# Four layers of a graph transformer on one core: the last target products of a GATv2 layer moved into the next, edge fields fetched a group sooner, and weight loads placed behind gathers

## The chip, the cores and the metric

The kernel runs on one core of one Trainium2 chip. The metric is device time in microseconds (us), the median of three runs. Everything is computed in 32-bit floating point; a matmul of such numbers is made of two passes of TensorE.

The engines are named as in the profile: PE is TensorE (PEld its weight loads), DVE is VectorE, ACT is ScalarE, POOL is GpSimd and SP is SyncE, which here only issues transfers. SP, ACT and POOL each issue DMAs, and each works through its instructions in order.

## The reference

A graph of 1,250 nodes with 512 features each and 21,250 edges goes through four layers. Each layer adds a graph part (gnn) and an attention part (mix) to x, and then a mixture of experts (ffn). The four layers differ in kind. This is the end of the reference, with arguments left out:

```python
xn = layernorm(x)
x = x + L0_gnn(xn, ...) + L0_mix(xn, ...)
x = x + L0_ffn(layernorm(x), ...)
xn = layernorm(x)
x = x + L1_gnn(xn, ...) + L1_mix(xn, ...)
x = x + L1_ffn(layernorm(x), ...)
...
xn = layernorm(x)
x = x + L3_gnn(xn, ...) + L3_mix(xn, ...)
x = x + L3_ffn(layernorm(x), ...)
```

Three of its pieces are touched by the change. `L0_gnn` is itself a stack of three GATv2 layers (k = 0, 1, 2), which the text calls GAT layers 0, 1 and 2:

```python
for k in range(Wl.shape[0]):
    xl = x @ Wl[k] + bl[k]
    xr = x @ Wr[k] + br[k]
    ef = ea2 @ We[k]
    m = jax.nn.leaky_relu(xl[src2] + xr[dst2] + ef, SLOPE)
    logit = m @ att[k]
    alpha = _segment_softmax(logit, dst2, n)
    out = jax.ops.segment_sum(xl[src2] * alpha[:, None], dst2, num_segments=n) + b_out[k]
    h = out + x
    ...                                   # layernorm of h, scaled by gamma, shifted by beta
    x = jax.nn.relu(h)
```

`L1_mix` is a global attention with the weights Wq, Wk, Wv, W1 and W2. `L3_gnn` is a graph convolution (`h = x @ W`, gathered by edge, weighted and summed by target), and `L3_mix` a linear attention whose projection `w_qkv` is three matrices of 512 x 512:

```python
q = softmax(x @ Wq.T) * dim ** -0.5       # L1_mix
k = softmax(x @ Wk.T, axis=-2)
x = einsum(q, einsum(k, x @ Wv.T)) + x
return x @ W1.T @ W2.T + x
...
q, k, v = split(x @ w_qkv.T, 3)           # L3_mix, per head
q = elu(q * SCALE) + 1; k = elu(k) + 1
out = einsum(q, einsum(k, v)) / (einsum(q, k.sum(axis=2)) + 1e-08)
return out @ w_out.T + b_out
```

The mixture of experts at the end of layer 0 writes its experts' outputs to a table in memory, from which every node gathers two rows; that of layer 2 does so too.

## The kernel before

**Nodes and edges.** The nodes are ten tiles of 128 rows (NT = 10). For the GAT layers they are also cut into twelve blocks of 107 (BN, NB). The edges (with a second self loop for each node) are sorted by target into 188 edge tiles of 128 (FT). Four tiles make a group (GE), so there are 47 groups (FG), about four to a block.

**A GAT layer** (`gat_layer`, L1209). Two tables in memory hold the products of the nodes with Wl (by source, `tl`, shown as xl) and Wr (by target, `tr`, shown as xr, stored as two halves of reduced precision). For an edge tile i, step i of the loop does the following.

- `load` gathers the source rows of a whole group by indirect DMA on POOL (L231), three groups ahead. At the start of a block it also loads the block's target rows, on SP.
- `fields` loads for a group a compressed table of targets, nb, and the edge attributes into the lower rows of the tile oh, both on SP, two groups ahead. There are four buffers of nb and three of oh.
- `onehot` (L1273, ACT) makes from nb the matrix that picks the target of each edge, one group ahead.
- `right` (L1286, L1287, PE) multiplies that matrix with the target rows into a PSUM bank. `logits` adds the source rows (L1299, DVE, the tile s) and reduces with the attention vector (L1302). For part of the tiles PE adds the source rows instead.
- `spread` makes one row of logits per group (z). When a block is full, `turn` (L1340, L1343) and `mix` (L1353, PE, bank `more`) sum the weighted source rows of the block.

A finished block is normed (L1371 to L1403, DVE and ACT), stored (L1096), transposed by `across` (L1409, L1415), and for every node tile that is then complete the two products of the *next* layer are queued in `late`: `gat_tables` has four matmuls with Wl (L1166), the copy on ACT (L1171), a reduction on DVE (L1182, `left`) and the store to tl (L1184); then four with Wr, a copy (L1174), a subtraction (L1188, `right`) and the store to tr (L1189). They use the PSUM bank called `tab`; `right` uses three banks called `mm`. The queues `todo`, `edge` and `late` give one piece of work to each step of the loop; after the last edge tile a loop empties them.

`prepare` loads the vectors of the layer and the weights of the next layer. It is moved on by one piece every third step, from step 6.

**The frame.** The order of instructions on an engine is not that of the source: a scheduler orders each engine's instructions by its own simulated times, transfers included, unless a part is marked to keep its written order. Buffers come from pools, and an instruction that reuses a buffer waits for its last reader.

```python
    def weight(self, src, k, n):
        w = self.wp.tile([128, k, n], F32, tag="w", name="w")
        self.nc.sync.dma_start(w, src.rearrange("(k p) n -> p k n", p=128))
        return w
```

This helper (L138) loads a weight of 512 x 512, 1 MB, on SP (L141).

**The end of layer 0's ffn** (`layer0_ffn`). Each expert's output tile is stored on ACT's queue (L1781, 256 KB, l0moe_out); then 20 gathers (L231, tile g) fetch two rows per node, `add_scaled` adds them to x (L1811), and `norm_tile` and `transpose_tile` prepare the input of layer 1. The next function, `global_attention` (L1814), begins with the loads of WkT, WvT, WqT and W1.

**The start of layer 3** (`layer3_attn`, L2929). `tail_steps` (L2377) gathers the two expert rows per node of layer 2 (routed_out, tile g, added to z at L2887), norms, scales (L2896 on ACT, L2897 on POOL), adds to x, norms again and transposes (L2386, L2388), tile by tile. Beside it run the products with gnn_W (L171), whose results are scaled (L2945) and stored as gcn_h (L2946) for the gathers of the graph convolution. `linear_attention_steps` (L734) loads the three parts of w_qkv and scales wq on ACT (L762).

Of the kernel before, what the change touches and what calls it, by code (L numbers as in the profile page):

```python
# [24 lines left out]
D = 512  # L25
NT = 10
# [31 lines left out]
class Net:  # L58
# [76 lines left out]
        else:  # L135
            self.nc.vector.tensor_copy(out, psum)

    def weight(self, src, k, n):  # L138

        w = self.wp.tile([128, k, n], F32, tag="w", name="w")  # L140
        self.nc.sync.dma_start(w, src.rearrange("(k p) n -> p k n", p=128))  # L141
        return w

# [588 lines left out]


    def linear_attention_steps(self, xn, xT, w_qkv, w_out, b_out, qscale, finish, added=None,  # L734
                               need=None):

# [10 lines left out]

        with self.tc.tile_pool(name="la", bufs=1) as p, \  # L750
                self.tc.tile_pool(name="latmp", bufs=2) as tmp:
            wk = self.weight(w_qkv[:, D:2 * D], 4, D)
            wv = self.weight(w_qkv[:, 2 * D:3 * D], 4, D)
            bo = self.rowvec(b_out)

            P = p.tile([128, 4, D], F32, name="P")
            ks = p.tile([128, D], F32, name="ks")
            for half in range(2):
                if half:
                    wq = self.weight(w_qkv[:, 0:D], 4, D)  # L760
                    if qscale != 1.0:
                        nc.scalar.mul(wq, wq, qscale)  # L762
# [24 lines left out]
            kv = tmp.tile([128, D], F32, tag="r", name="kv")  # L787
            for f in range(4):
                fs = slice(f * 128, (f + 1) * 128)
                m = self.mm([128, 128])  # L790
                for c in range(4):
                    nc.tensor.matmul(m, lhsT=wv[:, c, fs], rhs=P[:, c, fs], start=c == 0,
                                     stop=c == 3)
                nc.vector.tensor_tensor(kv[:, fs], m, self.pair, op=ALU.mult)
            for f in range(4):
                m = self.mm()
                nc.tensor.matmul(m, lhsT=kv[:, f * 128:(f + 1) * 128], rhs=wo[:, f, :],
                                 start=True, stop=True)
                self.evac(kvo[:, f, :], m)
            yield  # L800
            Q, QT = {}, {}
            for i in range(NT + 2):
                if i < NT:
                    r = rows(i)
                    nc.gpsimd.tensor_tensor(self.x[:r, i, :], self.x[:r, i, :], bo[:r],
                                            op=ALU.add)
                    q = tmp.tile([128, D], F32, tag="q", name="q")
                    phi(q, self.nat(xT, wq, i))
                    prod = tmp.tile([128, D], F32, tag="r", name="prod")
                    nc.vector.tensor_tensor(prod, q, ks, op=ALU.mult)  # L810
                    den = tmp.tile([128, 8], F32, tag="den", name="den")
                    nc.vector.tensor_reduce(den, prod.rearrange("p (h d) -> p h d", h=8), AX.X,
                                            ALU.add)
                    finish(den, den)
                    nc.vector.reciprocal(den, den)
                    q8 = q.rearrange("p (h d) -> p h d", h=8)
                    nc.vector.tensor_tensor(q8, q8, den.unsqueeze(2).to_broadcast([128, 8, 64]),
                                            op=ALU.mult)
                    Q[i] = q
                if 1 <= i <= NT:  # L820
                    qT = tmp.tile([128, 4, 128], F32, tag="qT", name="qT")
                    self.transpose_tile(qT, Q.pop(i - 1))
# [386 lines left out]
    def gat_layer(self, L, p, xtab, otab, big):  # L1209
# [25 lines left out]
        edge = deque()  # L1235
        late = deque()
        step = [0]

        def block(g):
            return g // 4, g % 4, g % 4 == 3 or g == FG - 1  # L1240
# [12 lines left out]
            G.setdefault(g, {})["xl"] = xl  # L1253

        def fields(g):
            nb = p.tile([128, GE * 128], BF16, tag="nb", name="nb", bufs=4)
            nc.sync.dma_start(nb, self.nbt[g])
            s = p.tile([128, GE * 128], F32R, tag="oh", name="oh", bufs=3)
            nc.sync.dma_start(s[BW:K].bitcast(F32),
                              self.eat[:, g * GE * 128:(g + 1) * GE * 128])  # L1260
            G.setdefault(g, {}).update(nb=nb, s=s)
# [99 lines left out]
        def finish(b):  # L1361
# [44 lines left out]
            def across():  # L1406
# [8 lines left out]
                    nc.scalar.copy(X[t][:, :, lo - t * 128:hi - t * 128],  # L1415
                                   q[:, :, lo - r0:hi - r0])
                for t in whole:
                    for f in self.gat_tables(nxt, p, t, lambda c, t=t: X[t][:, c, :],
                                             lambda: self.bank("tab", [128, D])):
                        late.append((step[0] + 1, f))  # L1420

            def add(t):
# [33 lines left out]
        for g in range(3):  # L1456
            load(g)
        fields(1)
        onehot(0)
        prepared = prepare()  # L1460
        for i in range(FT + 3):
            g, j = divmod(i, GE)
            step[0] = i
            if j == 1:
# [3 lines left out]
                    load(g + 3)  # L1468
                if g + 1 < FG:
                    onehot(g + 1)  # L1470
            if j == 2 and g + 2 < FG:
                fields(g + 2)
            if i >= 6 and i % 3 == 0:
                next(prepared, None)
            if i % 16 == 8 and i < FT:
                load_cur(i // 16)
# [15 lines left out]
            if late and late[0][0] <= i and (i % 2 == 0 or len(late) > 8):  # L1492
                late.popleft()[1]()
        bias_cur(NB - 1)
        while edge or todo or late:
            for _ in range(2):
                if edge:
# [32 lines left out]
    def layer0_ffn_to_layer1_attn(self):  # L1530
# [11 lines left out]
        with self.tc.tile_pool(name="l1a", bufs=1) as p:  # L1542
            xnT = p.tile([128, 4, NP], F32, name="xnT")
            with self.tc.tile_pool(name="l1b", bufs=1) as pb:
                xn = pb.tile([128, NT, D], F32, name="xn")
                with self.weights(), self.psum(3, 2, 3) if fast else self.psum():
                    count_pool()
                    self.counting = self.count_blocks(range(CB), True) if fast else iter(())
                    self.layer0_ffn(xn, xnT)
# [7 lines left out]
                    self.global_attention(xn, xnT, steps)  # L1557
                    for _ in steps:
                        pass
            count_ctx.close()  # L1560
# [88 lines left out]
    def layer0_ffn(self, xn, xnT):  # L1649
# [6 lines left out]
        with self.tc.tile_pool(name="l0f", bufs=1) as p, \  # L1656
# [113 lines left out]
            for e in range(8):  # L1770
# [3 lines left out]
                while (done + 1) * 128 <= (e + 1) * RM:  # L1774
# [5 lines left out]
                    self.evac(o.rearrange("p (f d) -> p f d", f=4), q)  # L1780
                    nc.scalar.dma_start(obuf[done * 128:(done + 1) * 128, :], o)  # L1781
                    done += 1
            for t in range(NT):
                for j in range(2):
                    g = tmp.tile([128, D], F32, tag="g", name="g", bufs=6)
                    self.gather(g, obuf[:, :], getI[:, t, j:j + 1])
                    self.add_scaled(t, g, G[:, t, j:j + 1])
                self.ready(t)
                self.norm_tile(t, xn[:, t, :])
                self.transpose_tile(xnT[:, :, t * 128:(t + 1) * 128], xn[:, t, :])  # L1790
                self.count(1)
            g1.close()

    def clear(self, p):

# [15 lines left out]
        self.nc.vector.scalar_tensor_tensor(x, psum[:r], gate[:r], x, op0=ALU.mult, op1=ALU.add)  # L1811


    def global_attention(self, xn, xnT, steps):  # L1814


        nc, I = self.nc, self.I
        with self.tc.tile_pool(name="ga", bufs=3) as big, \
# [26 lines left out]
            wv = self.weight(I["L1_mix_WvT"], 4, D)  # L1845
            P = large([128, NT, D])
            for f in range(4):
                c = self.mm()
# [1080 lines left out]
    def layer3_attn(self):  # L2929
        nc, I = self.nc, self.I  # L2930
        added = self.both_added()
        with self.tc.tile_pool(name="l3", bufs=1) as p:
            xnT = p.tile([128, 4, NP], F32, name="xnT")
            xn = p.tile([128, NT, D], F32, name="xn")
            need = self.tail_steps(xn, xnT)
            th = self.dram.tile([NP, D], F32, name="gcn_h")
            H = self.dram.tile([NP, D], F32, name="gcn_sum")
            dinv = self.dinv
# [9 lines left out]
            with self.tc.tile_pool(name="gcn", bufs=2) as tmp:  # L2948
# [3 lines left out]
                else:  # L2952
# [2 lines left out]
                steps = self.linear_attention_steps(  # L2955
                    xn, xnT, I["L3_mix_w_qkvT"], I["L3_mix_w_outT"], I["L3_mix_b_out"], 0.125,
                    lambda o, d: nc.vector.tensor_scalar(o, d, 1e-8, None, op0=ALU.add),
                    added)

                W, HL = {}, {}  # L2960

# [296 lines left out]
```

## Time and profile before

| | us |
|---|---|
| median of 3 runs | 4464.39 (4461.85 to 4471.24) |
| profiled execution, own time | 4489.82 |
| profiled execution, span | 4487.9 |
| PE busy | 3922.2 (87%) |
| DVE busy | 2689.5 (60%) |
| ACT busy | 1622.8 (36%) |
| POOL busy | 1351.0 (30%) |
| first gather of GAT layers 0, 1, 2 | 319.7, 758.6, 1184.8 |

The profile is one execution, and it was slower than the median of the runs. Busy shares are means over stages that are very different: the GAT layers keep PE busy nearly throughout, while PE stands still where one layer's gathers wait for the stores of the layer before. A row of the timeline gives the start, the busy time of the instruction or of a run of like ones, engine, line, operation, the tile written and the tiles read, the count, and in brackets how long the engine had been idle and what ended that. The granted clock is the share of full speed that TensorE was allowed; at 0.50 a pass takes twice as long.

### The profile page before, as it was taken

To read this page: it belongs to the slowest core of one execution; us is meant where nothing else is said; L and a number is where in the kernel's file an instruction comes from. 1 tells how busy PE (TensorE), PEld (TensorE's weight loads), DVE (VectorE), ACT (ScalarE), POOL (GpSimd) and SP (SyncE) were. 2 spreads that over 40 slices of the span, in tenths; PEclk is the share of its full clock that TensorE was granted. 3 is DMA by queue.
4 is the path that set the end of the run, shared out by engine and by line. 5 is a ranking of instruction groups with operands and counts; after the bars stand their busy time and mean duration, and the time that the engine had idled before them with its cause. 6 is when DMAs were issued, how large, how long until landed. Compare 5 with 4: busy or idle time off the path is not lost. (4 is left out here: it accounts for less than half of the span.)

```text
span 4487.9 us, 49486 instructions
## 1 busy us (share of the span) xinstructions
PE 3922.2 (87%) x15466; PEld 2415.7 (54%) x15466; DVE 2689.5 (60%) x6338; ACT 1622.8 (36%) x2976; POOL 1351.0 (30%) x1308
## 2 busy tenths in 40 slices
PE   5987998899788867799999999997979896898796
PEld 3434554455354434444788877563546562455474
DVE  5357895888398865523896767314584225687301
ACT  2222442344133375110464446223451232554121
POOL 2017773776466501102000000103131013675102
PEclk9988999999899988899999999999989998997798
DMA  6437664666466423402421110383002653666695
GB/s 220 159 84 211 198 199 150 198 197 193 141 179 189 145 74 108 119 17 64 146 70 42 46 35 29 143 298 128 12 27 83 233 189 119 182 200 199 225 339 181
DMA packets 283001, 647.58 MB, mean 144 GB/s; under 512 B 61673, under 2 KB 108905, under 8 KB 267322
## 3 DMA queue, kind: packets, MB, share of 16 engines
q1 hardware_dynamic: 169290, 357.13, 24.1%
q0 software_dynamic: 73088, 234.75, 18.3%
q10 hardware_dynamic: 40352, 52.44, 3.4%
q8 instruction: 127, 2.08, 0.2%
q14 instruction: 144, 1.18, 0.1%
HBM read 528.87 MB, written 120.65 MB: 145 GB/s over the span
## 5 line engine op out<-in xcount | busy, mean ns | idle before, releaser
L231 POOL DMA_INDIRECT xl<-xl,srcI x564 | 616.8, 1094 | 290.2 <-issue 137.8
L1353 PE MATMUL more<-xl,wT 128*128 128x512 f32 x1128 | 579.7, 601 | 14.5 <-ACT wT L1343 14.0
L1286 PE MATMUL mm<-hl,oh 121*128 121x512 f32 x564 | 419.1, 743 | 73.8 <-DVE s L1299 37.8
L1302 DVE SCALAR_TENSOR_TENSOR junk<-s,att 128x512 f32<-128x512 f32 x534 | 417.9, 783 | 6.8
L1299 DVE TENSOR_TENSOR s<-xl,mm 128x512 f32<-128x512 f32 x534 | 357.8, 679 | 104.0 <-PE mm L1287 48.4
L2129 PE MATMUL more<-hh,e 128*128 128x259 f32 x1600 | 383.7, 385 | 11.7 <-ACT o L2072 8.6
L2129 PEld LDWEIGHTS more<-hh,e 128*128 128x128 f32 x1600 | 295.1, 191 | 75.8 <-issue 17.8
L171 PE MATMUL mm<-w,xnT 128*128 128x512 f32 x640 | 307.8, 620 | 16.6 <-ACT xnT L2388 12.1
L231 POOL DMA_INDIRECT hs<-gcn_h,srcI x188 | 214.6, 1142 | 93.6 <-issue 30.8
L1353 PEld LDWEIGHTS more<-xl,wT 128*128 128x128 f32 x1128 | 196.1, 192 | 74.8 <-issue 27.9
L1287 PE MATMUL mm<-hl,oh 121*128 121x512 f32 x564 | 236.4, 419 | 0.0
L1286 PEld LDWEIGHTS mm<-hl,oh 121*128 121x128 f32 x564 | 111.0, 197 | 215.5 <-issue 117.1
L231 POOL DMA_INDIRECT g<-routed_out,getI x60 | 67.6, 1126 | 488.5 <-DMA routed_out<-o 416.4
L2049 ACT ACTIVATE e<-r,hh 128x512 f32<-128x512 f32 (+1 forms) x240 | 154.2, 646 | 130.7 <-PE more L2129 119.5
L171 PEld LDWEIGHTS mm<-w,xnT 128*128 128x128 f32 x640 | 123.4, 198 | 144.0 <-issue 124.6
L3011 PE MATMUL more<-hl,oh 128*128 128x512 f32 x376 | 161.5, 534 | 30.9 <-DVE oh L2975 10.9
L1273 ACT ACTIVATE oh<-nb 112x512 fp32r<-112x512 bf16 x141 | 88.7, 630 | 273.6 <-DMA nb<-nbt 162.3
L2052 ACT ACTIVATE e<-r,a 128x512 f32<-128x512 f32 (+1 forms) x240 | 152.3, 646 | 71.1 <-DVE e L2054 57.8
L711 PE MATMUL more<-ohs,ohb 128*128 128x512 bf16 x564 | 137.5, 383 | 42.8 <-ACT ohs L695 18.0
L2054 DVE TENSOR_TENSOR e<-e,e 128x512 f32<-128x512 f32 (+1 forms) x240 | 141.5, 596 | 51.2 <-ACT e L2049 44.8
L1287 PEld LDWEIGHTS mm<-hl,oh 121*128 121x128 f32 x564 | 112.4, 199 | 110.1 <-issue 108.4
L1166 PE MATMUL tab<-w,xT 128*128 128x512 f32 x320 | 163.5, 605 | 9.0 <-ACT xT L1415 6.1
(631 smaller groups left out, 7787.8 us busy)
## 6 DMA issues: line engine op xcount, KB each, us to landing
w<-L_ffn_Wp SPq DMA_DIRECT2D x64, 1024.0 KB
w<-L_ffn_table SPq DMA_DIRECT2D x56, 1025.0 KB
neg<-ntab SPq DMA_DIRECT2D x80, 320.0 KB
nb<-nbt SPq DMA_DIRECT2D x141, 128.0 KB
hl<-xr SPq DMA_DIRECT2D x36, 448.0 KB
xr<-tro SPq DMA_DIRECT2D x30, 512.0 KB
xe<-routed_in SPq DMA_DIRECT2D x56, 256.0 KB
routed_out<-o ACTq DMA_DIRECT2D x56, 256.0 KB
```

The source lines that it names most:

```text
L171: self.nc.tensor.matmul(p, lhsT=xT[:, c, t * 128:(t + 1) * 128], rhs=w[:, c, n0:n0 + n], start=c == 0, stop=c == k - 1)
L231: self.nc.gpsimd.indirect_dma_start(out=out, out_offset=None, in_=table, in_offset=bass.IndirectOffsetOnAxis(ap=idx, axis=0), bounds_check ...
L1166: nc.tensor.matmul(d[name], lhsT=xT(c), rhs=L[name][:, c, :], start=c == 0, stop=c == 3)
L1286: nc.tensor.matmul(m, lhsT=s, rhs=hl[:K, 0, :], start=True, stop=False)
L1287: nc.tensor.matmul(m, lhsT=s, rhs=hl[:K, 1, :], start=False, stop=not on_pe(i))
L1299: nc.vector.tensor_tensor(o, d["xl"][:, j, :D], s, op=ALU.add)
L1302: nc.vector.scalar_tensor_tensor(junk, s, 0.0, L["att"], op0=ALU.max, op1=ALU.mult, accum_out=d["lg"][:, j:j + 1])
L1353: nc.tensor.matmul(B[b]["y"], lhsT=d["wT"][:, j, :], rhs=d["xl"][:, j, :D], start=k == 0 and j == 0, stop=last and j == GE - 1)
L2049: nc.scalar.activation(e1[:, :n], R[q, k, 0][:, :n], AF.Exp, bias=HH[q][:, s, 256:257])
L2052: nc.scalar.activation(e2[:, :n], R[q, k, 1][:, :n], AF.Exp, bias=heads[q][0][:, s, 0:1])
L2129: nc.tensor.matmul(ys[j], lhsT=e[:, j * 128:(j + 1) * 128], rhs=HH[q][:, s, :], start=s == 0, stop=s == NT - 1)
L3011: nc.tensor.matmul(y, lhsT=oh, rhs=hl[:, i], start=i + j == 0 and not (self.fast and k), stop=last and i + j == GE)
```

## The change

There are four parts.

1. In GAT layers 0 and 1, for the last three node tiles (t = 7, 8, 9) only the product with Wl is queued at once. The product with Wr, its copy, subtraction and store go into a list `rest`, which the next layer works off after its first gathers, fields and one-hot are issued and before its first `right`. After the last edge tile the products use `mm` banks instead of `tab`.
2. `fields` runs three groups ahead instead of two, with one more buffer of each kind, and `prepare` is moved on from step 15 instead of 6.
3. At the end of layer 0's ffn WkT is loaded before the gathers and WvT behind them. "Behind" means that POOL first writes one element of the weight's buffer; the load then waits for POOL to come to that point. POOL's order is kept as written here. WqT and W1 are loaded as before, in the order of the source, without such a write.
4. At the start of layer 3 the three parts of w_qkv are loaded behind, after the first tile of the tail.

```diff
-    def weight(self, src, k, n):
+    def weight(self, src, k, n, behind=False):
         w = self.wp.tile([128, k, n], F32, tag="w", name="w")
+        if behind:
+            self.nc.gpsimd.memset(w[:1, 0, :1], 0.0)
         self.nc.sync.dma_start(w, src.rearrange("(k p) n -> p k n", p=128))
...
     def linear_attention_steps(self, xn, xT, w_qkv, w_out, b_out, qscale, finish, added=None,
-                               need=None):
+                               need=None, ws=None):
...
+            if ws is None:
+                wk = self.weight(w_qkv[:, D:2 * D], 4, D)
+                wv = self.weight(w_qkv[:, 2 * D:3 * D], 4, D)
+            else:
+                wk, wv, wq = ws
...
         def fields(g):
-            nb = p.tile([128, GE * 128], BF16, tag="nb", name="nb", bufs=4)
+            nb = p.tile([128, GE * 128], BF16, tag="nb", name="nb", bufs=5)
             nc.sync.dma_start(nb, self.nbt[g])
-            s = p.tile([128, GE * 128], F32R, tag="oh", name="oh", bufs=3)
+            s = p.tile([128, GE * 128], F32R, tag="oh", name="oh", bufs=4)
...
                 for t in whole:
-                    for f in self.gat_tables(nxt, p, t, lambda c, t=t: X[t][:, c, :],
-                                             lambda: self.bank("tab", [128, D])):
+                    fs = self.gat_tables(nxt, p, t, lambda c, t=t: X[t][:, c, :],
+                                         lambda: self.mm() if ending[0] else
+                                         self.bank("tab", [128, D]))
+                    if t >= NT - 3:
+                        rest.extend(fs[5:])
+                        fs = fs[:5]
+                    for f in fs:
                         late.append((step[0] + 1, f))
...
         fields(1)
+        fields(2)
         onehot(0)
+        for f in L.pop("rest", ()):
+            f()
         prepared = prepare()
...
-            if j == 2 and g + 2 < FG:
-                fields(g + 2)
-            if i >= 6 and i % 3 == 0:
+            if j == 2 and g + 3 < FG:
+                fields(g + 3)
+            if i >= 15 and i % 3 == 0:
                 next(prepared, None)
...
         bias_cur(NB - 1)
+        ending[0] = True
...
+        if nxt is not None:
+            nxt["rest"] = rest
         return nxt
...
-            for t in range(NT):
-                ...
+            wk = self.weight(I["L1_mix_WkT"], 4, D)
+            with self.tc.manual_schedule(engines={mybir.EngineType.Pool}):
+                for t in range(NT):
+                    ...
+                wv = self.weight(I["L1_mix_WvT"], 4, D, behind=True)
             g1.close()
+        return wk, wv
...
-    def global_attention(self, xn, xnT, steps):
+    def global_attention(self, xn, xnT, ws, steps):
-            wk = self.weight(I["L1_mix_WkT"], 4, D)
+            wk, wv = ws
...
-    def tail_steps(self, xn, xnT):
+    def tail_steps(self, xn, xnT, behind=None):
...
+                if t == 0 and behind is not None:
+                    behind()
...
-            need = self.tail_steps(xn, xnT)
+            ws = []
+
+            def load():
+                ws.extend(self.weight(I["L3_mix_w_qkvT"][:, i:i + D], 4, D, behind=True)
+                          for i in (D, 2 * D, 0))
+
+            need = self.tail_steps(xn, xnT, load)
```

More of the change, by code (lines that the diff above doesn't have):

```diff
@@ L751, in linear_attention_steps @@
                 self.tc.tile_pool(name="latmp", bufs=2) as tmp:
-            wk = self.weight(w_qkv[:, D:2 * D], 4, D)
-            wv = self.weight(w_qkv[:, 2 * D:3 * D], 4, D)
+            if ws is None:
[3 more added lines that the diff above has]
+                wk, wv, wq = ws
             bo = self.rowvec(b_out)
@@ L759, in linear_attention_steps @@
                 if half:
-                    wq = self.weight(w_qkv[:, 0:D], 4, D)
+                    if ws is None:
+                        wq = self.weight(w_qkv[:, 0:D], 4, D)
                     if qscale != 1.0:
@@ L1237, in gat_layer @@
         step = [0]
+        rest = []
+        ending = [False]
         def block(g):
@@ L1548, in layer0_ffn_to_layer1_attn @@
                     self.counting = self.count_blocks(range(CB), True) if fast else iter(())
-                    self.layer0_ffn(xn, xnT)
+                    ws = self.layer0_ffn(xn, xnT)
                     self.count(NB * 16)
@@ L1556, in layer0_ffn_to_layer1_attn @@
                         steps = self.count_steps()
-                    self.global_attention(xn, xnT, steps)
+                    self.global_attention(xn, xnT, ws, steps)
                     for _ in steps:
@@ L1782, in layer0_ffn @@
                     done += 1
-            for t in range(NT):
[L1784 to L1791, printed above, removed]
+            wk = self.weight(I["L1_mix_WkT"], 4, D)
+            with self.tc.manual_schedule(engines={mybir.EngineType.Pool}):
+                for t in range(NT):
+                    for j in range(2):
+                        g = tmp.tile([128, D], F32, tag="g", name="g", bufs=6)
+                        self.gather(g, obuf[:, :], getI[:, t, j:j + 1])
+                        self.add_scaled(t, g, G[:, t, j:j + 1])
+                    self.ready(t)
+                    self.norm_tile(t, xn[:, t, :])
+                    self.transpose_tile(xnT[:, :, t * 128:(t + 1) * 128], xn[:, t, :])
+                    self.count(1)
+                wv = self.weight(I["L1_mix_WvT"], 4, D, behind=True)
             g1.close()
+        return wk, wv
     def clear(self, p):
@@ L1843, in global_attention @@
                 next(steps, None)
-            wv = self.weight(I["L1_mix_WvT"], 4, D)
             P = large([128, NT, D])
@@ L2957, in layer3_attn @@
                     lambda o, d: nc.vector.tensor_scalar(o, d, 1e-8, None, op0=ALU.add),
-                    added)
+                    added, ws=ws)
                 W, HL = {}, {}
```

## The prediction

> **What bounds the kernel now.** I read the page's busy shares first, then windows around the places that the diff touches, then the timeline there, then the list of waits.
>
> ```profile
> PE 3922.2 (87%) x15466; PEld 2415.7 (54%) x15466; DVE 2689.5 (60%) x6338; ACT 1622.8 (36%) x2976; POOL 1351.0 (30%) x1308
> 700.00:741.00 41.00, 41.00 (x124) 19.75 (x123) 13.80 (x33) 13.02 (x25) 2.70 (x3) 1.00 0.24 80
> ```
>
> The second line (us, then busy time and count of PE, PEld, DVE, ACT, POOL, then granted clock, DMA share, GB/s) is the end of GAT layer 0: PE is busy in all 41 us, DVE in 14. There TensorE sets the end, so a product taken out of it is worth its own time. The next rows are the change of layer, 0 to 1:
>
> ```profile
> 741.34 0.75 DVE L1371 SCALAR_TENSOR_TENSOR h<-more,r,c 103x512 f32<-103x512 f32 x1 [6.47 <-issue]
> 745.97 0.57 PE L1409 MATMUL tp<-ident,h 103*128 103x103 f32 x4 [2.46 <-ACT h L1403]
> 747.23 3.70 PE L1166 MATMUL tab<-w,xT 128*128 128x512 f32 x8 [0.69 <-ACT xT L1415]
> 752.31 0.33 SPq L1184 DMA_DIRECT2D xl<-tlo  x1
> 752.34 3.70 PE L1166 MATMUL tab<-w,xT 128*128 128x512 f32 x8 [1.41 <-DVE junk L1182]
> 758.60 1.03 POOL L231 DMA_INDIRECT xl<-xl,srcI  x1 [12.22 <-DMA xl<-tlo]
> 764.96 0.69 DVE L1299 TENSOR_TENSOR s<-xl,mm 128x512 f32<-128x512 f32 x1 [7.57 <-DMA xl<-xl,srcI]
> ```
>
> The last block's norm starts when the last mix ends (741.34); its transpose follows, then tile 9's left product (747.23), its store, and only when that has landed the first gather. The right product of tile 9 (752.34) already runs beside that landing. So the path is mix, norm, transpose, left product, store, gather. From layer 1 to 2 it is the same, but slower in one row:
>
> ```profile
> 1173.23 6.38 PE L1166 MATMUL tab<-w,xT 128*128 128x512 f32 x8 [0.59 <-ACT xT L1415]
> 1184.78 1.03 POOL L231 DMA_INDIRECT xl<-xl,srcI  x1 [12.63 <-PE tab L1166]
> 1188.58 0.69 DVE L1299 TENSOR_TENSOR s<-xl,mm 128x512 f32<-128x512 f32 x1 [2.51 <-DMA xl<-xl,srcI]
> ```
>
> **Part 1, target products left to the next layer.** One product of 128x512 is two passes; eight passes take 3.70 us, spaced 0.43, so a product is 0.86. In the order of the changed kernel 9 products instead of 16 stand between the transpose of block 10 and the last mix: 7 x 0.86 = 6.0 us off a stretch where PE is the bound. The last mix should end 6.0 earlier at both changes of layer.
>
> What is late next is the clock. Before, the tail of products and six rights of the next layer (741.54 to 743.5) filled the start of the norm's wait. Now both stand behind the twelve products left over, and PE has nothing for some 4.7 us (741.3 to 745.97).
>
> ```profile
> 1168.42:1171.83 3.41, 0.94 (x5) 0.47 (x4) 2.53 (x7) 0.91 (x3) 1.34 (x1) 1.00 0.71 246
> 1171.83:1175.25 3.42, 2.83 (x7) 1.48 (x8) 0.00 (x0) 0.50 (x1) 0.32 (x1) 0.50 0.81 176
> 741.75:745.17 3.42, 1.75 (x7) 0.94 (x5) 3.31 (x8) 0.79 (x2) 0.36 (x1) 1.00 0.49 172
> ```
>
> A stretch of 3.41 us with PE busy for 0.94 was followed by half clock (0.50), one with 1.75 was not. The Trainium skill, page "TensorE: Matmul & The Clock Gate", Part 1, has the clock halved after a wholly idle window of about 3.4 us, the windows running free. By that rule an idle of 4.7 holds such a window with a chance of (4.7 - 3.41) / 3.41 = 0.38, and the first change of layer keeps nearly its 6.0. By the row, a window that is 28% busy is enough, and in 4.7 us of idleness one window is always that poor. I take the row: tile 9's left product then takes 6.38 instead of 3.70 at the first change (2 to 2.7 lost; the second pays it already). First gather: -4 at the first (range -1 to -7), -6 at the second.
>
> The twelve products left (10.3 us at 0.86) run from the end of the left product, and the first right can only follow. At the first change this time was covered: 764.96 - 750.93 = 14.0 us to the first sum s. At the second it was 1188.58 - 1179.6 = 9.0, so 10.3 and a right of 0.8 sticks out by 2; gathers run ahead meanwhile, and the lag is caught up in part, since a gather comes each 1.32 us and the sums need less. Two more tiles' stores (1 MB) and their ACT casts and DVE subtractions (0.59 and 0.69 each) fall into that wait. SP stands at the load of Wr until the twelve are done, and behind it tile 9's store and the edge rows of later groups. Net -4 (range 0 to -7) and -5 (range -1 to -7).
>
> **Part 2, fields three groups ahead.**
>
> ```profile
> ACT oh L1273 <- DMA nb<-nbt: 162.3, 68, 11.9
> ```
>
> This is a long wait (total, times, longest), but of an engine with slack: group 5's one-hot of layer 1 was written at 787.9 and its first right began at 803.2; group 4's at 781.1 and 790.3. So the wait does not bind where I followed it. Prepare's loads and weights come nine steps later, on queues that are then no longer full. I take -1 over three layers (range -8 to +1: SP issues in order, so a group's fields that wait for a buffer hold up the next block's target rows behind them; the one buffer more of each kind keeps that wait where it was, and if it did not, one gather's 1.32 us is the price).
>
> **Part 3, end of layer 0's ffn.**
>
> ```profile
> 1809.24 0.81 ACTq L1781 DMA_DIRECT2D l0moe_out<-o  x2
> 1815.83 1.05 POOL L231 DMA_INDIRECT g<-l0moe_out,getI  x1 [62.05 <-DMA ctab<-acc]
> 1820.00:1832.00 12.00, 1.31 (x5) 0.97 (x6) 9.77 (x22) 0.41 (x2) 9.69 (x10) 0.50 0.79 182
> ```
>
> The gathers wait for the last output tile to land, 1809.66 to about 1814.9, 5.3 us, with up to 4 MB of weights beside it; at the very end of the kernel such a tile lands in 2.95. Three of the four weights go behind: about -2. But only Wv has the memset that holds it until 20 gathers are issued; Wq stands ahead of it on SP with nothing to wait for, and comes as 1 MB beside the first gathers, where the DMA share is 0.79: 1 MB at 377 GB/s is 2.8 us, in 12 x 0.21 = 2.5 free ones and 4.2 x 0.43 before them: +1.5. POOL's order is now written out; it stays as it was. The memset itself is one element on a queue that then has only 1.1 us of work in 12; the weight's buffer has been free since the last expert's products, so it waits for nothing. Net -0.5 (range -2 to +2).
>
> **Part 4, start of layer 3.**
>
> ```profile
> 3729.03 0.33 ACTq L2367 DMA_DIRECT2D routed_out<-o  x1
> 3736.03 1.05 POOL L231 DMA_INDIRECT g<-routed_out,getI  x1 [54.80 <-DVE oh L2975]
> 3745.23 1.91 ACT L762 ACTIVATE w<-w 128x2048 f32<-128x2048 f32 x1 [0.19 <-DMA g<-routed_out,getI]
> 3729.00:3736.00 7.00, 0.00 (x0) 0.00 (x0) 0.73 (x5) 1.28 (x1) 0.00 (x0) 0.70 1.01 377
> 3757.00:3770.00 13.00, 10.54 (x21) 4.19 (x21) 9.44 (x30) 3.85 (x9) 11.11 (x10) 0.79 0.64 181
> ```
>
> Four weights (4 MB) fill the queues (share 1.01) while the last output tile lands in 6.2 us. Three leave: landing in about 2.95, so gathers start 3.3 earlier. Their three memsets stand on POOL behind gather 10 (near 3759, now 3756); 3 MB at 377 GB/s want 8.3 us of DMA, and 13 x 0.36 = 4.7 are free: the later gathers slip by up to 3.6, of which DVE (9.4 of 13 busy) absorbs some. The scaling of wq (1.91 us of ACT, in idle time before) moves 22 instructions back and waits for the third load (my estimate: landed 3768 to 3776); behind it on ACT stand the roots of the norms, which DVE needs, and the copies of xnT, which PE needs. At the end the transposes of the last two tiles now stand together ahead of 16 products; these are the same passes in another order, which I put at 0 (-3 to +2), since the store of gcn_h after the last of them comes after all of them either way. Net -2 (range -8 to +5).
>
> **Sum**: -4 - 5 - 1 - 0.5 - 2 = -12.5 us. The profiled execution took 4489.8, 25.4 above the median of 4464.4; the sum is a difference within it and I carry it over unchanged: 4452. A difference under 0.2% (8.9 us) can't be told from none.
>
> **Rivals.**
> - Fields do bind. From first gather to the weighted rows z of group 3 the layers take 53.4, 44.9 and 49.6 us, where 16 gathers of 1.32 and some 4 us of landing make 25. If waits on SP for fields are behind that, three groups ahead gives about 8 a layer: 24 more, 4428. Against it: one-hots stand ready well before their rights. Chance 0.2.
> - Waits only change places: half clock at both changes (3 gained), the twelve products ahead of the first rights (2), nothing from the weights: -5, 4460. Chance 0.2.
> - Slower: weights behind gathers slow the gathers. The Trainium skill's "DMA: Bandwidth & Descriptors", "Issuing engines are not separate DMA queues", says that transfers of all engines share the same 16 and interleave. If mixed traffic moves only the 182 GB/s of the row at 1820 instead of 377, 3 MB of weights and 2.6 MB of gathers in layer 3 need 31 us instead of 14: gathers and ACT at L762 are 14 to 17 late; 2 MB at the other end add 5 to 8. That is +22 less the 10 of part 1 and 2: 4476. It decides when the third load of layer 3 lands after about 3790. Against it is the start of layer 1, where gathers and a weight together moved 351 GB/s. Chance 0.1.
>
> ```profile
> 758.60:765.00 6.40, 0.00 (x0) 0.00 (x0) 0.04 (x1) 0.00 (x0) 5.06 (x5) 0.52 1.00 351
> ```
>
> - The change does not do all that it says: Wq is not held back; that is in the sum.
>
> **How the numbers follow.** Likeliest (0.5): -9 to -18, at 4452. With the fields' case (0.2) faster by over 0.2% has 0.7; the swap's case and the weak half of the likeliest, 0.2 within; slower 0.1. The range runs from 4430, which takes in most of the fields' case and a layer 3 at its best end, to 4466.
>
> **What would show it.** Right: 16 passes and more of L1166 in a row after each L1409 of the last block; last mix to first gather longer than 17.3 at the first change, with 0.50 granted over tile 9's left product; first gathers of layers 1 and 2 about 4 and 9 earlier than before, measured from layer 0's; last output to first gather of layer 3 near 4. Wrong: from first gather to group 3 shorter by over 5 us (fields bind), L762 with a long wait on DMA w, or a last store of gcn_h later than before by that distance (weights slow the gathers).

## The result and the profile after

Over eight runs of each, the changed kernel took 4450.46 us (4445.45 to 4456.67) and the kernel before 4462.48 (4459.49 to 4471.24): a ratio of 0.9971, 95% interval 0.996 to 0.9981, or 12.9 us less, between 8.5 and 17.9. The forecast was 12.5 less.

The two profiled executions are 38.8 us apart (spans 4487.9 and 4449.1), three times the difference of the medians. The first profile of before was an unusually slow execution, so no stage below is read from that pair alone: distances within a stage are taken from several profiles of each kind. Line numbers differ a little between the kernels: L1166, L1371 and L1409 of the kernel before are L1172, L1379 and L1417 in the changed one.

The change of layer 0 to 1 after the change, in the timeline (start, busy, engine, line, operation, operands, count, idle before and what ended it):

```profile
729.91 0.75 DVE L1379 SCALAR_TENSOR_TENSOR h<-more,r,c 103x512 f32<-103x512 f32 x1 [3.04 <-issue]
734.03 0.87 PE L1417 MATMUL tp<-ident,h 103*128 103x103 f32 x4 [4.21 <-ACT h L1411]
735.50 16.71 PE L1172 MATMUL mm<-w,xT 128*128 128x512 f32 x32 [0.59 <-ACT xT L1423]
743.29 0.33 SPq L1190 DMA_DIRECT2D xl<-tlo  x1
750.34 1.03 POOL L233 DMA_INDIRECT xl<-xl,srcI  x1 [15.67 <-DMA xr<-tro]
752.24 0.38 SPq L143 DMA_DIRECT2D w<-L_gnn_Wr  x1
754.46 0.69 DVE L1307 TENSOR_TENSOR s<-xl,mm 128x512 f32<-128x512 f32 x1 [4.34 <-DMA xl<-xl,srcI]
```

The windows (us, busy time and count of PE, PEld, DVE, ACT and POOL, granted clock, DMA share, GB/s):

```profile
729.00:734.50 5.50, 1.29 (x5) 0.47 (x4) 3.26 (x7) 0.83 (x2) 1.09 (x1) 0.97 0.29 73
734.50:738.00 3.50, 2.91 (x6) 1.26 (x5) 0.00 (x0) 0.50 (x1) 0.17 (x1) 0.50 0.58 161
```

All 16 products (32 passes) stand in one row behind the last transpose. TensorE has been idle for 4.21 us before it, and the first products run at the half clock (0.50): tile 9's table row is stored 8 us after its first product, and the twelve others end at 752.2, before the rows of the first gather have landed, as forecast. With them the last use of the old Wr ends, and SP sends the load of the next one (752.24). In the list of waits (total, times, longest), the wait for fields did not shrink (162.3 before):

```profile
ACT oh L1281 <- DMA nb<-nbt: 210.7, 82, 17.3
```

At the end of layer 0's ffn and at the start of layer 3, in the timeline and, after it, in one window each:

```profile
1779.07 0.81 ACTq L1800 DMA_DIRECT2D l0moe_out<-o  x2
1783.23 1.05 POOL L233 DMA_INDIRECT g<-l0moe_out,getI  x1 [56.01 <-issue]
1787.37 0.43 SPq L143 DMA_DIRECT2D w<-L_mix_WqT  x1
```

```profile
1791.00:1803.00 12.00, 2.09 (x8) 1.43 (x8) 8.54 (x22) 0.40 (x2) 8.35 (x8) 0.50 1.01 264
```

```profile
3705.34 0.33 ACTq L2389 DMA_DIRECT2D routed_out<-o  x1
3708.36 1.05 POOL L233 DMA_INDIRECT g<-routed_out,getI  x1 [50.89 <-DVE oh L3005]
3731.31 0.14 POOL L142 MEMSET w<- 1x1 f32 x3
3731.43 1.48 SPq L143 DMA_DIRECT2D w<-L_mix_w_qkvT  x3
3748.21 1.89 ACT L768 ACTIVATE w<-w 128x2048 f32<-128x2048 f32 x1
```

```profile
3731.00:3744.00 13.00, 9.40 (x20) 3.59 (x18) 10.31 (x27) 3.27 (x8) 10.15 (x13) 0.87 0.94 348
```

Wq comes 4 us after the first gather, beside the others, and the DMA share reads 1.01. In layer 3 the first gather follows the last output by 3.0 us instead of 7.0; three weights go out behind gather 10, and with the gathers beside them 348 GB/s were moved. The scaling of wq (L768) shows no idle time before it: the third load had landed.

### The profile page after: what moved, and what is told of

The parts are those of the page before. It is cut to its first block, busy times and chain, and to the rows that moved or that the text cites. A ratio compares the mean times of both kernels' runs of the same rounds, so it can differ in the third digit from the quotient of the medians.

```text
span 4449.1 us, 49465 instructions
## 1 busy us (share of the span) xinstructions
PE 3910.9 (88%) x15466; PEld 2413.9 (54%) x15466; DVE 2683.3 (60%) x6338; ACT 1621.5 (36%) x2976; POOL 1348.4 (30%) x1312
## 4 chain that ended last, share of the span: by engine, by line
PE 32%; DVE 8%; DMA 6%; issue 4%; ACT 2%; POOL 2%; SPq 0%; POOLq 0%; ACTq 0%; DVEq 0%
PE more L2151 5%; PE mm L2014 4%; PE mm L181 3%; PE mm L173 3%; PE mm L3203 2%; DMA xe<-routed_in 2%; PE mm L782 2%; PE mm L2384 2%; PE mm L2379 2%; PE more L2717 2%; PE mm L2717 1%; PE mm L2113 1%; PE more L3041 1%; DVE junk L2042 1%; DVE e L2076 1%
## 5 line engine op out<-in xcount | busy, mean ns | idle before, releaser
L2151 PE MATMUL more<-hh,e 128*128 128x259 f32 x1600 | 382.2, 384 | 11.7 <-ACT o L2094 8.7
L1361 PEld LDWEIGHTS more<-xl,wT 128*128 128x128 f32 x1128 | 196.1, 193 | 85.4 <-ACT wT L1351 36.6
L3001 ACT ACTIVATE hl<-hs,rec 128x512 fp32r<-128x512 f32 x188 | 130.5, 718 | 87.7 <-PE more L3041 43.0
```

Of the source, the lines that this page charges most:

```text
L1361: nc.tensor.matmul(B[b]["y"], lhsT=d["wT"][:, j, :], rhs=d["xl"][:, j, :D], start=k == 0 and j == 0, stop=last and j == GE - 1)
L2151: nc.tensor.matmul(ys[j], lhsT=e[:, j * 128:(j + 1) * 128], rhs=HH[q][:, s, :], start=s == 0, stop=s == NT - 1)
```

## The experiments

Ratios are to the kernel before in the same group of runs. There are four groups: the result, the single parts, and two of variants. The kernel before took 4462, 4473, 4499 and 4510 us in them, so times of different groups are not set side by side. Distances are from start to start; the last mix is the last pass of L1353 ahead of a change of layer. "First gather to z" is the distance from a GAT layer's first gather to the row of logits of a group, read from the timeline.

**Before again.** No edit.

> The kernel before, unchanged, for a second profile. The first profile of before took 4489.8 us, 27 more than the median of its runs, and stood still for 5 to 8 us at a time in places where several engines show an idle time that nothing released (layer 0 at 340 to 353, layer 3 at 3843 to 3857). If those are chance, this profile's span is near 4461 and the first-gather-to-z distances of group 3 are shorter than 53.4, 44.9 and 49.6 us in some layers. If they belong to the kernel, the span is near 4488 again and the distances repeat within 2 us.

4467.12 us, span 4465.3. From first gather to z of group 3 the three layers took 53.5, 36.6 and 36.1 us, so 13.5 of layer 2's 49.6 and 8.3 of layer 1's 44.9 in the first profile belong to that execution. So do 9 in layer 3, where from the last output to the last gather of the graph convolution it is 379.7 us against 388.6. At the change of layer 0 to 1 its timeline also shows what the first profile did not:

```profile
749.95 6.50 PE L1166 MATMUL tab<-w,xT 128*128 128x512 f32 x8 [0.59 <-ACT xT L1415]
```

The left product took 6.50 us here, without any change, where the first profile has 3.70. At the second change of this profile the window before the half clock has TensorE busy for 1.42 of 3.41 us:

```profile
1168.64:1172.05 3.41, 1.42 (x7) 0.81 (x5) 3.06 (x8) 0.99 (x3) 0.65 (x1) 1.00 0.58 211
```

And in layer 0 fields do bind:

```profile
358.63 0.63 ACT L1273 ACTIVATE oh<-nb 112x512 fp32r<-112x512 bf16 x1 [21.61 <-DMA nb<-nbt]
359.31 0.80 PE L1286 MATMUL mm<-hl,oh 121*128 121x512 f32 x1 [6.37 <-ACT oh L1273]
```

TensorE waited 6.4 us for a one-hot, and that for a field 21.6. In the first profile other idle time lay over this place.

**Part 1 alone.**

```diff
+                    if t >= NT - 3:
+                        rest.extend(fs[5:])
+                        fs = fs[:5]
```

> Part 1 alone: target products of tiles 7, 8, 9 left to the next layer; fields, prepare and weights as before. Theory of the prediction: -9 us (about -6 at each last mix, 3 given back at the first change by the half clock, 1 to 2 at the second by the twelve products ahead of the first right). Rival, that the start of a layer takes it all back: 0.

Ratio 0.9976 (0.9964 to 0.9987), 10.7 us less. From the last group's z to the last mix both layers take 27.4 us, in all four profiles without the part 33.1: 5.7 less twice, against 6.0 forecast.

**Part 2 alone.**

```diff
-            if j == 2 and g + 2 < FG:
-                fields(g + 2)
-            if i >= 6 and i % 3 == 0:
+            if j == 2 and g + 3 < FG:
+                fields(g + 3)
+            if i >= 15 and i % 3 == 0:
```

> Part 2 alone: fields three groups ahead with one buffer more, prepare from step 15. Theory of the prediction: the one-hot's wait does not bind, -1 us (range -8 to +1). Rival, that the fields bind at the starts of layers, as the two profiles suggest where z of group 3 came 15, 11 and 15 us sooner: -20 or more. A third: the starts are shorter and the gain is given back some groups later, as layer 0 shows by group 6: -1 to -6.

Ratio 0.9992 (0.998 to 1.0003), 3.6 us less and not told apart from none. In its profile layer 0 has z of group 3 at 39.8 us (53.5 before), and of group 4 at 57.8 (60.6): most is given back at once. The changed kernel shows the same, and why:

```profile
373.76 0.62 ACT L1135 CAST wehl<-we 3x512 fp32r<-3x512 f32 x1 [8.12 <-POOL we L1132]
375.14 1.11 PE L1348 MATMUL tp<-ident,z 128*128 128x128 f32 x4 [14.96 <-ACT z L1332]
```

A cast of `prepare` (L1135) waits on ACT for a result of POOL; behind it stand the exps of the first block, and TensorE waits 15 us for them. The rival of 20 us or more is refuted; the third case, a gain given back some groups later, fits.

**Parts 3 and 4 alone.** The edits of those parts, without the others.

> Parts 3 and 4 alone: Wk before and Wv behind the gathers of layer 0's end, the three parts of w_qkv behind those of layer 3. Theory of the prediction: -2.5 us. From the two profiles: first gathers -2.4 and -4.0, of which +3.9 and +0.7 are given back by the end of the gathers: -2. Rival, that weights beside gathers cost more than they bring: +5 or more.

Ratio 0.998 (0.9971 to 0.9989), 9 us less, more than forecast. Distances in us, as ranges over the profiles (with the parts: this one, after, and the six later ones in which one weight stands beside the gathers of layer 0; without: the first profile, its repetition and the two single parts above; line numbers are those of the kernel before):

| | without | with |
|---|---|---|
| last l0moe_out issued to first gather | 6.2 to 7.7 | 3.4 to 3.7 |
| first gather to the 20th addition (L1811) | 36.9 to 38.0 | 39.9 to 41.1 |
| last l0moe_out to the 20th addition | 43.0 to 45.7 | 43.6 to 44.5 |
| last routed_out of layer 2 to first gather | 6.9 to 7.1 | 3.0 |
| first gather to the 20th z (L2887) | 51.4 to 53.2 | 52.5 to 53.3 |
| last routed_out to last gcn_h issued | 88.3 to 90.0 | 81.9 to 85.0 |

Layer 3 gains 4.0 us at its first gather, loses 0.7 in the gathers on the means, and 2.3 more come by the last store. The end of layer 0 loses nearly all that it gains.

**The idle time filled.** In the changed kernel, tile 7's four products are put before the last transpose, where TensorE stands still.

```diff
             def across():
+                if b == NB - 1:
+                    for f in rest[:5]:
+                        f()
+                    del rest[:5]
                 q = self.tp([128, 4, R])
```

> The changed kernel, with the four products of tile 7 (its part of the rest) put between the last mix and the last transpose, where TensorE otherwise stands still for 4 us. If the half clock after that idle time costs what the trace of after shows (tile 9's left product 6.4 us instead of 3.7), last mix to first gather becomes about 17 to 18 us instead of 21.1 at the first change and 17.2 at the second, and the kernel gains 3 to 6 us on the changed one. Rival, that the clock is lost in any case by the phase of its windows, as the two profiles of before show (17.9 and 21.7 at the same place): within 2 us of the changed kernel.

Ratio 0.9955 (0.9944 to 0.9966), where the changed kernel itself got 0.9974 in the same group, 8.5 us more. The timeline and a window of the same place:

```profile
736.39 0.57 PE L1421 MATMUL tp<-ident,h 103*128 103x103 f32 x4 [0.78 <-ACT h L1411]
737.66 10.57 PE L1172 MATMUL mm<-w,xT 128*128 128x512 f32 x24 [0.69 <-ACT xT L1427]
748.26 0.38 SPq L143 DMA_DIRECT2D w<-L_gnn_Wr  x1
749.56 1.04 POOL L233 DMA_INDIRECT xl<-xl,srcI  x1 [12.60 <-PE mm L1295]
756.42 0.69 DVE L1307 TENSOR_TENSOR s<-xl,mm 128x512 f32<-128x512 f32 x1 [6.85 <-DMA xl<-xl,srcI]
```

```profile
734.50:738.00 3.50, 2.03 (x8) 0.87 (x7) 1.83 (x4) 1.61 (x3) 1.27 (x1) 1.00 0.51 162
```

The clock stays at 1.00. From tile 9's xT to its tlo, the time of the left product and its surroundings, it is 4.29 us at both changes of layer, in this and in all three later kernels with the filling (8 of 8). In the five profiles with the rest and no filling it is 5.68 to 7.00 (10 of 10). In the four without the rest it is 4.29 twice and 5.99 to 7.09 six times. From the last mix to the first sum s the second change gains: 18.8 us against 22.0 to 23.3. The first does not: its gather starts 3 us sooner, but the first sum follows by 6.9 instead of 3.8 to 4.5. The rows show what stands in between. The load of Wr (1 MB) goes out when the last product left over has ended; with eight left instead of twelve that is 1.3 us before the first gather, and with twelve it was 1.9 us after it. All thirteen profiles agree at this change: where the load goes out 1.3 to 3.7 us ahead of the first gather (seven profiles), the first sum follows the gather by 5.0 to 7.1 us; where it goes out 1.5 to 2.1 us behind (six), by 3.8 to 4.5. No run changed that order alone. So 3.5 of the 8.5 us between this kernel and the changed one have a place; for the others I have none.

**Wq behind too.**

```diff
                 wv = self.weight(I["L1_mix_WvT"], 4, D, behind=True)
+                wq = self.weight(I["L1_mix_WqT"], 4, D, behind=True)
```

> The changed kernel, with WqT also loaded behind the gathers of layer 0's end instead of beside them. The changed kernel's gathers take 40.1 and 40.5 us from the first gather to the last addition, those of three profiles without the change 37.6 to 38.0. If the 1 MB beside them is the reason, this becomes about 38 and the kernel gains 2 us; rival, that it is POOL's written order: still 40.

Ratio 0.9972 (0.9963 to 0.998), gathers to the last addition 40.0. This did not test the expectation: the load of W1 moved up into the place.

```profile
1809.97 0.38 SPq L143 DMA_DIRECT2D w<-L_mix_W  x1
```

It went out 4.2 us after the first gather, as Wq had.

**Prepare's small work on POOL.** The cast L1135 and the stores of the table ends are issued by POOL itself.

```diff
-        nc.scalar.copy(hl[:3, 0], v[:3])
+        nc.gpsimd.tensor_copy(hl[:3, 0], v[:3])
...
-        nc.sync.dma_start(L["ends"][8:9], hl[2:3].bitcast(F32))
+        nc.gpsimd.dma_start(L["ends"][8:9], hl[2:3].bitcast(F32))
```

> The changed kernel, with the small work of the next layer's weights (the cast of the edge weights, from ACT, and the stores to the table ends, from SP) issued by POOL, which makes their inputs. Theory: in layers 0 and 1 the fields' gain is given back by waits for POOL that stand on ACT and SP ahead of the first block's exp and of later fields (PE waits 15 us for z in layer 0, 6 us for wT in layer 1). Then z of group 4 in layer 0 comes at about 45 us after the first gather instead of 58, z of group 6 in layer 1 near 53 instead of 60, and the kernel gains 5 to 15 us on the changed one. Rival, that the starts are bound by transfers or by the loading of code: within 3 us, z of later groups the same.

Ratio 0.9993 (0.9982 to 1.0004): worse than the changed kernel, by about 5 us between the medians; where they are lost was not found. The exps no longer wait for the cast, and z of group 4 in layer 0 came at 58.0 us, where the changed kernel in the same group has 63.4; but by group 5 it is 71.9 against 72.3, and by group 12 123.3 against 122.4. In that group the changed kernel (its second profile, below) waits ahead of the place that I wanted to mend, and TensorE waits 4.1 us for the exp there instead of 15. So the theory fell; whether it holds where the starts are free of other idle time was not tried.

**The changed kernel again.** No edit.

> The changed kernel itself, beside its variants on one chip and for a second profile. Its parts alone summed to -23 us (rest -10.7, fields -3.6, weights -9); the whole was -12 to -13. If the parts overlap, as layer 1 of the two profiles hints (first gather to z of group 46: 372.9 with both, 369 to 371 with none or one), -13 again; if that was the spread between chips, -18 to -23.

Ratio 0.9974 (0.9965 to 0.9983), 11.7 us less. So the whole is 12 to 13 in both of its groups, and the parts' sum of 23 overlaps with that only at the edge of its errors. But the parts and the whole were never run in one group; the parts ran on one chip and this repetition on another, so a difference between chips is not excluded. Its profile has the starts of layers full of idle time such as this, in layer 0:

```profile
358.47 0.69 DVE L1307 TENSOR_TENSOR s<-xl,mm 128x512 f32<-128x512 f32 x1 [9.84 <-remote]
```

From first gather to z of group 3 it takes 54.8, 48.8 and 51.5 us in the three layers, where its first profile has 38.4, 33.9 and 34.3.

**Filled, and no weight beside the gathers.** Wq and W1 both behind.

```diff
-                wv = self.weight(I["L1_mix_WvT"], 4, D, behind=True)
+                wv, wq, w1 = (self.weight(I["L1_mix_" + n], 4, D, behind=True)
+                              for n in ("WvT", "WqT", "W1"))
```

> e5_fill with WqT and W1 both behind the gathers of layer 0's end, so that no weight stands beside them (in e6_wq_behind W1 had moved into the place of WqT: it was issued 4 us after the first gather). If 1 MB beside the gathers is why they take 40.0 to 40.7 us instead of 37.6 to 38.0, now 37.5 to 38.5, and 2 us less than e5_fill. Rival, POOL's written order or work of VectorE that has not moved: 40 again, and the time of e5_fill, 0.9955 of before.

Ratio 0.9945 (0.993 to 0.996), the best of all, though its interval overlaps that of the filling alone.

```profile
1840.43 0.14 POOL L142 MEMSET w<- 1x1 f32 x3
```

The three weights now wait behind the last gather (the three writes at 1840.43). With nothing beside them the gathers take 38.7 us to the last addition (40.2 in the filled kernel), and 42.4 from the last output. So one weight beside the gathers costs about 1.5 us, by this one profile. The forecast was 37.5 to 38.5: about 1 us of the longer gathers is left, and POOL's written order is not excluded as its cause.

**Filled, without part 2.** Fields two groups ahead, prepare from step 6.

> e5_fill with part 2 undone (fields two groups ahead, one buffer less of each kind, prepare from step 6). If the fields are worth the 3.6 us that they showed alone, ratio to before 0.996, from layer 0, whose distance from first gather to z of group 20 rises by 5; rival, that in the presence of the rest they bring nothing or cost: 0.9955 or less.

Ratio 0.995 (0.9935 to 0.9965). No loss shows without the fields, but with six runs a loss of 3.6 us could not be seen: the interval is 7 us to either side. The distance to z of group 20 in layer 0 is 186.1 us, in two kernels of its group with the fields 184.9 and 185.7, so the 5 us forecast for it did not come.

**Filled, four tiles in the rest.**

```diff
-                    if t >= NT - 3:
+                    if t >= NT - 4:
```

> e5_fill with four node tiles instead of three in the rest (one xT buffer more); the products of tile 6 now fill the gap before the last transpose and tiles 7, 8 and 9 run in the next layer, as in the changed kernel. Theory: another four products leave the stretch that TensorE bounds, 3.4 us at each change of layer: z of group 46 to the last mix 3 less than 27.4, of which the twelve products at the start give back 0 to 2: 3 to 6 us better than e5_fill, 0.9945. Rival, that the starts of the layers take it all: 0.9955.

Ratio 0.9952 (0.9936 to 0.9967), not told apart from three tiles. The stretch from the last z to the last mix is 26.1 us, only 1.3 less than 27.4. TensorE is busy there all but 0.5 us (0.3 with three tiles), so it is still the bound; but the stretch held 20 passes of products with three tiles put off and 16 with four. Only four passes (1.7 us) left it and not eight; the others had run before the last z already.

## Why the prediction was right

The sum held (12.5 forecast, 12.9 measured), but in part by luck. Each part alone brought more than its term: 10.7 us for 9, 3.6 for 1 and 9 for 2.5, each known to 4 or 5 us. Together they measured about half of those 23, and the forecast had simply added its terms. Terms that were too small met a whole that came out less than its parts; why it did is open (below).

- **The last mixes: right.** 5.7 us at each change of layer, for 6.0 forecast; the same in every profile with three tiles put off.
- **The half clock: the mechanism right.** Every unfilled change with the rest ran at half clock, and the filling removed it. It costs 1.4 to 2.7 us (5.68 to 7.00 from xT to tlo, for 4.29).
- **How poor a window must be.** The clock of these traces changes at distances that are multiples of 3.41 us, so its windows can be laid over TensorE's work. At the 26 changes of layer in the thirteen profiles, half clock followed all 16 times that TensorE was busy for 42% or less of the poorest window (0 to 42%; the 1.42 of 3.41 us above is the upper end), and none of the 10 times that it was busy for 51% or more (the lower end is the row at 741.75 in the prediction). The rule of the Trainium skill ("TensorE: Matmul & The Clock Gate", Part 1), taken as a wholly idle window of about 3.4 us, gives as an estimate a chance of 0.38, or 0.23 for the 4.2 us measured. In the traces only two of the ten unfilled gaps hold such a window, and all ten were slowed. The claim that one window is always as poor as 28% was too strong: a gap of 4.2 us cut in half by the border of two windows leaves 38% in each. It was enough, because 42% is.
- **What the half clock cost the change: mis-sized.** I charged 2 to 2.7 us to the change because the one profile of before showed 3.70 at the first change. Three of four profiles without the rest pay it there too: the mean from xT to tlo is 6.0 us without the rest and 6.3 with it. The cost was already in the kernel.
- **Twelve products ahead of the first right: right at the second change, a gain missed at the first.** At the second change, from last mix to first sum, it is 22.6 us on the mean of five profiles against 21.3 of four: 1.3 given back, for 2 forecast. At the first it is 24.5 against 26.1, so 1.6 gained. That fits the load of Wr, which the twelve products hold back until the first gather is out; the forecast had SP standing there until then, but put no gain on it. Part 1 comes to 7.3 us at the first change and 4.4 at the second by these readings, for 4 and 5.
- **Fields: the size right, the reading wrong.** I found that the wait does not bind. In layer 0 it does (6.4 us of TensorE), hidden in the first profile by other idle time. The sign of being wrong that I had named, group 3 sooner by over 5 us, came in layer 0 with part 2 alone and in the first profile of the changed kernel (39.8 and 38.4 us for 53.5), and was gone in its second (54.8). Part 2 brought 3.6 us alone (-9 to +1), and nothing that its removal from the filled kernel could show. I take it that the next thing is late there, exps behind prepare's cast or other idle time; the run that moved the cast did not show it. The rival of 24 us is refuted. (Two starts of rights in the forecast were misread: those of groups 4 and 5 of layer 1 are 790.0 and 801.3, and the slack of 8 and 13 us stays.)
- **End of layer 0: the net right, both of its terms too small.** On the means, first gather 3.5 us sooner (2 forecast) and 2.7 given back by the gathers (1.5 forecast), of which about 1.5 is the weight beside them. Net 0.7, for 0.5.
- **Start of layer 3: mis-sized.** 4.0 at the first gather (3.3 forecast). The price of 3 MB beside the gathers was put at up to 3.6 us and measured as 0.7: 348 GB/s went through, and ACT did not wait for wq. Between the 20th z and the last store, where the order of the last tiles was put at 0, another 2.3 were gained; that the order is their cause was not tested. So 5.6 and not 2; the rival of slower gathers, which needed 182 GB/s, is refuted.

What is open: the parts alone come to 23 us and the whole to 12 or 13; even the readings by stage above (11.7 for part 1, 0.7 and 5.6 for the weights) are more than the whole. Layers 1 and 2 of the changed kernel's first profile are 2 to 4 us longer from first gather to the last z than with part 1 or part 2 alone, but the same distance varies by as much between kernels that are alike there, and in the later groups by 9.

## What to carry to other kernels

One profile tells the order of work, not its typical size: a clock state or a stall in it may be the luck of that execution, so a second profile of the kernel before is worth more than a finer reading of the first. When work is taken out of a bound stretch, ask what fills the idle time that follows; here four products moved into a gap of 4 us kept the clock up, and that kernel took 8.5 us less than the changed one, of which 3.5 have a place in the traces. Ask also which transfer the last product of such a stretch lets go: here it was a weight that went out ahead of the first gather, and the first change of layer gained nothing. Holding loads back by a write to their buffer works, but whatever is next on the queue moves up into their place.

## What was not expected of the hardware

Partly busy windows are enough for the half clock: at the changes of layer it followed every time that TensorE had been busy for 42% or less of a window of 3.41 us, and never at 51% or more. A gap of 4.2 us always leaves such a window. Without the rest the gap is 2.5 us in one piece, and whether it leaves one goes by where the border of the windows falls (24 to 42% in six changes of layer, 51% in two), so the same code was 3 us apart there from one execution to the next. And the starts of the GAT layers differ by 15 to 17 us between the two profiles of the changed kernel, and by 0 to 13.5 between those of the kernel before, with several engines idle at once and no releaser but "issue" or "remote"; what holds them was not settled.
